# Layer 3 of a four-layer kernel: score copies by pairs of PSUM banks, softmax sums of the first sequence on TensorE, MLP steps regrouped

## The chip, the cores and the metric

The kernel runs on one core of a Trainium2 chip. A core has five engines that take their instructions in order, each from its own queue: TensorE (PE; its weight loads are listed apart as PEld), VectorE (DVE), ScalarE (ACT), GpSimd (POOL) and SyncE (SP), which here only issues DMAs. They wait for each other through semaphores. Data lie in SBUF (128 partitions) and in PSUM, which has eight banks of 2 KB per partition and takes the results of matmuls. The metric is the time of one execution on the device in microseconds (us), less being better. The kernel before took 3798.1 us, the median of three runs (3795.4 to 3805.48).

## The reference

Four layers in a row on x of shape 4 x 512 x 512 (four sequences of 512 positions): cross attention (layer 0), two recurrent layers (1 and 2), and layer 3, a resampler with an MLP. Everything is float32. The change is in layer 3:

```python
residual = latents                              # the output of layer 2, 4 x 512 x 512
h = concat([x, latents], axis=1)                # x is the context: 1024 keys per sequence
q = (latents @ q_w + q_b)                       # 16 heads of 32
kv = (h @ kv_w + kv_b)
attn = einsum('bkhd,bnhd->bhkn', q, kmat) / DH
attn = where(full_mask, attn, -inf)             # the mask is on the 512 context keys only
attn = softmax(attn)
attn_out = einsum('bhkn,bnhd->bkhd', attn, v) @ out_w + out_b + residual
out = rmsnorm(attn_out, postnorm_w)
out = gelu(out @ mlp_w1 + mlp_b1) @ mlp_w2 + mlp_b2     # 512 -> 2048 -> 512
return out + residual
```

## The kernel before, in words

Layers 0 to 2 fill the first 2398 us and are not touched, except that the pool of their weight buffers (`wpool`, four buffers of 8 KB per partition, line 36) is opened at the top of the kernel and is used by layer 3 too, through `load_w` (line 61).

Layer 3 (`layer3`, from line 1102) treats the four sequences b = 0 to 3 one after the other. The 16 heads of a sequence are four groups m of four heads. The four heads of a group sit in four row groups of TensorE and are computed together. A *unit* is (b, m, h), where h is one half of the 512 queries. The 1024 keys of a unit are eight blocks of 128, and a *turn* i works on two of them, so a unit has four turns (NS = 4), a group m has eight (PERIOD), a sequence 32, and there are 128 turns in all. In this text T0 to T3 are the turns i with i mod 4 = 0 to 3, and c = i mod 8 is the turn in its group.

The loop over turns (line 1414) is the order of work on TensorE, VectorE, ScalarE and GpSimd: nothing reorders it, each engine takes its own instructions in the order in which the loop writes them (`manual_schedule`), and semaphores follow from which tile an instruction reads or writes. SP's DMAs go as early as their buffers are free, in order. A turn has parts that belong to different blocks of keys, as a pipeline written out by hand:

- `scores(i)`: 16 matmuls (two per product in float32) into the PSUM tile `ps`, 4 x 2 x 256 columns, that is four banks, one for each head of the group. There is one such tile, so the next scores wait until all its readers are done.
- `largest(i)`: VectorE takes the maximum over the two blocks into `run`; on the first four blocks (the context) it adds the mask column `mc` as it does.
- `kept(i)`: ScalarE copies the scores to an SBUF tile `w` (six buffers), adding the mask column on the context blocks. It comes after `largest` and waits for it.
- In T0, for the unit that has just ended: `gathered` turns `run` on TensorE (`ptm`) and VectorE reduces it to `mx`; `spread` turns `mx` back over all partitions (`pb`) and ScalarE copies it to `mb`.
- `lowered(i-4)`: VectorE subtracts `mb` from `w`. `weights(i-4)`: ScalarE takes the exponential in place.
- a *tick*: VectorE writes a one-column tile and GpSimd copies it to `mark`, so that GpSimd does not pass that point earlier (lines 1449 to 1451).
- `added(i-5)`: GpSimd adds the two blocks of `w` to the accumulator `acc` (two buffers).
- `values(i-5)`: 16 matmuls of `w` with the values into `po`, one bank for both query halves.
- two turns after the last values of a unit: `counted` sums `acc` over the partitions with a matmul with ones (`pn`), and `divided` takes the reciprocal on VectorE and writes the result to `y`.

Beside these, a turn takes pieces of two generators (`taken`, line 1395). `early` prepares the next group: `prep` (projections q, k, k, v, v in five pieces), and, where the next group opens a new sequence, first `begin` (loads, four transposes `ptx` copied to `xT`, and four GpSimd additions of the output bias at line 1150). It runs at c = 0, 4 and 6, with two, two and three pieces. `rest` is `finish(b)`, the output projection, the norm and the MLP of the sequence before; it runs at the other five turns of a group, two pieces at a time. Its 38 pieces are: the output projection of each of four row tiles (`pout`), the normed transpose of a half of the rows (`ptn` to `nT`), and for each of two halves and four blocks of 512 hidden columns two pieces `ph` with gelu into `hT` (two buffers) and two pieces `po2` added to the residual. After four output pieces, the first `nT` shifts the pairs by one, so that in the first half of the rows a turn holds one `ph` and one `po2` piece or an `nT`, and in the second half both of a kind. When the last sequence's attention is done, the rest of its `finish` runs alone.

`ps_s` is a pool of three PSUM banks, used by everything that is neither `ps` nor `po`.

The instructions of `mm` (all projections and MLP matmuls) carry line 73, those of `columns` line 1293.

## Time and profile before

| what | value |
|---|---|
| median of three runs | 3798.1 us (3795.4 to 3805.48) |
| the profiled execution, its own time | 3804.08 us |
| its span, first to last instruction | 3802.2 us |
| mean granted TensorE clock | 0.95 |
| busy: PE, PEld | 3443.3 us (91%), 1972.7 us (52%) |
| busy: DVE, ACT, POOL | 2711.7 (71%), 1930.9 (51%), 1915.7 (50%) |
| layer 3 from its first scores | 2398.07 us to the end |

The span is what the engines' rows cover; the execution's own time is 1.9 us more. The page has the span in 40 slices of 95 us; a digit is the busy share in tenths. Times within layer 3 are given as us from the start of the span. In the rows of the timeline the columns are start, duration, engine, line, operation, the tile written and the tiles read, shapes and count, and in brackets the idle time before the instruction and the engine and tile that ended it. In the view of waits: who waited, for whom, us in total, times, longest.

### The profile page before, as it was taken

To read this page: it belongs to the slowest core of one execution; us is meant where nothing else is said; L and a number is where in the kernel's file an instruction comes from. 1 tells how busy PE (TensorE), PEld (TensorE's weight loads), DVE (VectorE), ACT (ScalarE), POOL (GpSimd) and SP (SyncE) were. 2 spreads that over 40 slices of the span, in tenths; PEclk is the share of its full clock that TensorE was granted. 3 is DMA by queue.
4 is the path that set the end of the run, shared out by engine and by line. 5 is a ranking of instruction groups with operands and counts; after the bars stand their busy time and mean duration, and the time that the engine had idled before them with its cause. 6 is when DMAs were issued, how large, how long until landed. Compare 5 with 4: busy or idle time off the path is not lost. (4 is left out here: it accounts for less than half of the span.)

```text
span 3802.2 us, 54498 instructions
## 1 busy us (share of the span) xinstructions
PE 3443.3 (91%) x21952; PEld 1972.7 (52%) x21952; DVE 2711.7 (71%) x3637; ACT 1930.9 (51%) x2758; POOL 1915.7 (50%) x1106
## 2 busy tenths in 40 slices
PE   9999999988999999999999977667789999989889
PEld 3333333465566666666666634334455555555456
DVE  6777777689988888888888861466666666566631
ACT  4777775534444444444444422355565566656531
POOL 4777776524444444444444432266654554554540
PEclk9999999999999999999999989688899999999999
DMA  4000000156677777777777764100022212212123
GB/s 151 24 12 23 12 9 20 34 146 142 147 178 177 178 187 178 177 178 177 174 176 177 180 155 103 43 10 23 15 71 88 81 45 92 67 59 73 62 94 122
DMA packets 188235, 385.75 MB, mean 101 GB/s; under 512 B 18064, under 2 KB 44816, under 8 KB 185936
## 3 DMA queue, kind: packets, MB, share of 16 engines
q1 hardware_dynamic: 149680, 250.67, 20.4%
q0 software_dynamic: 38304, 131.61, 19.0%
q8 instruction: 173, 2.83, 0.3%
q14 instruction: 78, 0.64, 0.1%
HBM read 246.45 MB, written 4.19 MB: 66 GB/s over the span
## 5 line engine op out<-in xcount | busy, mean ns | idle before, releaser
L292 POOL TENSOR_TENSOR aT<-aT,nmT 128x1536 f32<-128x1536 f32 x124 | 428.5, 3460 | 208.1 <-ACT aT L290 184.8
L1288 POOL TENSOR_TENSOR acc<-acc,w 128x1024 f32<-128x1024 f32 x192 | 491.5, 2560 | 7.8 <-POOL mark L1451 0.2
L254 DVE CUSTOM_DVE_ANT_0 sc<-psc,nm 128x512 f32<-128x512 f32 x512 | 354.1, 692 | 148.0 <-PE psc L242 90.3
L871 DVE TENSOR_TENSOR ry<-kv,o_r 128x1024 f32<-128x1024 f32 x256 | 397.7, 1594 | 7.2 <-PE pm L73 0.5
L1451 POOL COPY mark<-tick 128x1 f32<-128x1 f32 x128 | 92.7, 724 | 556.9 <-DVE tick L1450 378.1
L1276 ACT ACTIVATE w<-w 128x2048 f32<-128x2048 f32 x128 | 244.5, 1911 | 200.4 <-DVE w L1272 187.7
L1272 DVE TENSOR_TENSOR w<-w,mb 128x2048 f32<-128x2048 f32 x128 | 321.5, 2522 | 1.8 <-ACT mb L1265 1.8
L866 DVE TENSOR_TENSOR_SCAN kv<-W,kv 128x1032 f32<-128x1032 f32 x128 | 296.4, 2315 | 0.2 <-DMA kv<-A 0.2
L584 POOL DMA_DIRECT2D kv<-A x127 | 111.5, 878 | 360.6 <-DVE kv L839 227.6
L290 ACT COPY aT<-pst 128x512 f32<-128x512 f32 x372 | 196.5, 595 | 178.6 <-PE pst L279 178.1
L73 PE MATMUL ph<-nT,l_m 128*128 128x256 f32 x1024 | 240.7, 393 | 18.0 <-DVE nT L1357 18.0
L73 PE MATMUL po<-l_m,hT 128*128 128x512 f32 x512 | 238.2, 611 | 18.8 <-ACT hT L1374 18.8
L298 ACT ACTIVATE aT<-aT 128x2048 f32<-128x2048 f32 x128 | 246.8, 1929 | 5.6 <-POOL aT L292 4.9
L1293 PE MATMUL po<-w,v 128*32 128x256 f32 x2048 | 160.1, 437 | 84.4 <-ACT w L1276 48.3
L73 PEld LDWEIGHTS ph<-nT,l_m 128*128 128x128 f32 x1024 | 199.3, 197 | 61.9 <-DVE nT L1357 19.2
L279 PE MATMUL pst<-q,km 32*128 32x512 f32 x1024 | 206.5, 640 | 9.4 <-DVE mxs L254 5.8
L1236 DVE TENSOR_TENSOR run<-ps,run 128x1024 f32<-128x1024 f32 x128 | 156.5, 1223 | 77.4 <-PE ps L1199 75.2
L1199 PE MATMUL ps<-q,kT 32*128 32x256 f32 x2048 | 170.1, 453 | 40.2 <-ACT w L1220 32.5
L1383 DVE TENSOR_TENSOR x<-po,x 128x512 f32<-128x512 f32 x64 | 44.2, 691 | 223.3 <-PE po L73 223.3
L242 PE MATMUL psc<-km,q 32*128 32x512 f32 x1024 | 198.9, 653 | 0.8 <-ACT q L223 0.8
L1220 ACT ACTIVATE w<-ps,mc 128x1024 f32<-128x1024 f32 x128 | 135.6, 1110 | 118.0 <-DVE tick L1450 62.0
L885 PE MATMUL py<-ry,k 128*32 128x512 f32 x1024 | 161.6, 627 | 36.0 <-DVE ry L871 24.3
(268 smaller groups left out, 7311.8 us busy)
## 6 DMA issues: line engine op xcount, KB each, us to landing
l_m<-in_L_W SPq DMA_DIRECT2D x64, 1024.0 KB, 5.0
kv<-A POOLq DMA_DIRECT2D x127, 516.0 KB, 6.1
L_wk<-in_L_Wk SPq DMA_DIRECT2D x16, 1024.0 KB, 7.9
L_wr<-in_L_Wr SPq DMA_DIRECT2D x16, 1024.0 KB, 7.1
L_wv<-in_L_Wv SPq DMA_DIRECT2D x16, 1024.0 KB, 5.8
L_wg<-in_L_Wg SPq DMA_DIRECT2D x16, 1024.0 KB, 7.9
L_wo<-in_L_Wo SPq DMA_DIRECT2D x64, 256.0 KB, 4.9
L_fk<-in_L_fWk SPq DMA_DIRECT2D x16, 1024.0 KB, 6.6
```

Source lines behind the costliest of these rows:

```text
L73: nc.tensor.matmul(ps, lhsT, rhs, start=(i == 0), stop=(i == len(pairs) - 1))
L242: nc.tensor.matmul(psc, d["q"][g][rs, lt * P : (lt + 1) * P], d["km"][rs, a, :], start=True, stop=True, tile_position=(32 * r, 0),)
L254: nc.vector.tensor_tensor_reduce(sc, ps[r], d["nm"][lt], 1.0, -3.0e38, ALU.add, ALU.max, mxs[:, a, lt, c : c + 1])
L279: nc.tensor.matmul(pst, d["km"][rs, a, s * P : (s + 1) * P], d["q2", a][rs, :], start=True, stop=True, tile_position=(32 * r, 0),)
L290: nc.scalar.copy(w[:, r, :], pst)
L292: nc.gpsimd.tensor_tensor(w[:, n:, :], w[:, n:, :], nmT[:, None, :].to_broadcast([P, NR - n, L]), ALU.add)
L298: nc.scalar.activation(w, w, AF.Exp)
L866: nc.vector.tensor_tensor_scan(flat(kv), flat(W[g % 2]), flat(kv), 0.0, ALU.mult, ALU.add)
L871: nc.vector.tensor_tensor(y, kv[:, 4 * h : 4 * h + 4, None, :TP].to_broadcast([P, 4, 2, TP]), d["r"][:, i].rearrange("p (o m) -> p o m", o ...
L1272: nc.vector.tensor_tensor(w, w, mb, ALU.subtract)
L1276: nc.scalar.activation(w, w, AF.Exp)
L1288: nc.gpsimd.tensor_tensor(d["acc", m, h], d["acc", m, h], w[:, :, e, :], ALU.add)
```

## The change

- The tile `ps` is read by pairs of its four banks: `largest` takes two half maxima for each pair, and `kept` is called twice, for the upper pair ahead of `lowered` and `weights`, for the lower pair after `largest`. The copy no longer adds the mask; the exponential does, as a bias, on the context blocks. `w` has seven buffers.
- `scores` comes first in a turn, and `values` and `added` are a turn later (VAL is 6, not 5).
- In sequence 0 the exponentials are summed on TensorE: `values` has a second set of 16 matmuls with `ones` into `pn`, which is held through the unit; `added`, `counted` and the tick are left out there, and `divided` comes in the turn of the last values. In the other sequences `counted` and `divided` come seven turns behind the last scores, as before, with `counted` ahead of `values`; `acc` has one buffer.
- The pieces of `finish` are larger: two output projections, the first `nT`, and then a whole `ph` block (`hidden`) or a whole `po2` block (`closed`), one in a turn. The second `nT` follows the first `hidden`. In the last sequence the `hidden` of the next block comes ahead of `closed`. `hT` has one buffer (in the last sequence it takes buffers of `w`), `nT` two.
- Which turn takes which piece is written out in `turns` and `ready`: for sequences 1 to 3 `prep` at c = 0, 0, 4, 6, 6 (at 2, 2, 4, 6, 6 where the next sequence is begun; its `begin` is at c = -1 and 0, two transposes each), in sequence 0 at 1, 2, 4, 6, 7.
- `wpool` is opened later and closed with layer 2; layer 3 has its own three weight buffers (`wp`).

```diff
-    wpool = ctx.enter_context(tc.tile_pool(name="w", bufs=NW))
...
-                    if k % 2:
+                    if k == 1:
                         yield
                 for x in xn[b]:
                     nc.gpsimd.tensor_tensor(x, x, ob, ALU.add)
+                yield
...
-            def kept(i):
+            def kept(i, c):
+                (b, m, h), j = place(i)
+                if i not in ws:
+                    ws[i] = sp.tile([P, NR, 2, HQ], F32, tag="w", name="w", bufs=7)
+                nc.scalar.copy(
+                    ws[i][:, c : c + 2].rearrange("p r e q -> p (r e q)"),
+                    st[b]["ps"][:, c : c + 2].rearrange("p r e q -> p (r e q)"),
+                )
...
-                run = d["run"]
-                for e in range(2):
-                    mc = d["mc"][:, s + e : s + e + 1]
-                    if a:
-                        nc.vector.tensor_tensor(run, ps[:, :, e, :], run, ALU.max)
...
+                for c in range(0, NR, 2):
+                    ps, run = d["ps"][:, c : c + 2], d["run"][:, c : c + 2]
+                    for e in range(2):
+                        mc = d["mc"][:, s + e : s + e + 1]
+                        if a:
+                            nc.vector.tensor_tensor(run, ps[:, :, e, :], run, ALU.max)
+                        elif j or e:
+                            nc.vector.scalar_tensor_tensor(run, ps[:, :, e, :], mc, run, ALU.add, ALU.max)
+                        else:
+                            nc.vector.tensor_scalar(run, ps[:, :, e, :], mc, None, ALU.add)
...
+            def ticked(i):
+                if 0 <= i - VAL < NU and units[(i - VAL) // NS][0]:
+                    tick = sp.tile([P, 1], F32, tag="tick", name="tick")
+                    nc.vector.memset(tick, 0.0)
+                    nc.gpsimd.tensor_copy(mark, tick)
...
             def weights(i):
-                w = ws[i].rearrange("p r e q -> p (r e q)")
-                nc.scalar.activation(w, w, AF.Exp)
+                (b, m, h), j = place(i)
+                w = ws[i]
+                a, s = divmod(2 * j, LT)
+                if a:
+                    w = w.rearrange("p r e q -> p (r e q)")
+                    nc.scalar.activation(w, w, AF.Exp)
+                else:
+                    for e in range(2):
+                        nc.scalar.activation(
+                            w[:, :, e, :], w[:, :, e, :], AF.Exp, bias=st[b]["mc"][:, s + e : s + e + 1]
+                        )
...
-                    d["acc", m, h] = sp.tile([P, NR, HQ], F32, tag="acc", name="acc", bufs=2)
+                    d["acc", m, h] = sp.tile([P, NR, HQ], F32, tag="acc", name="acc", bufs=1)
...
+                if b == 0 and j == 0:
+                    d["pn"] = ps_s.tile([P, HQ], F32, tag="s", name="pn")
                 for e in range(2):
+                    ends = dict(start=(j == 0 and e == 0), stop=(j == NS - 1 and e == 1))
+                    columns(po[:, h, :], lambda r: v[:, 2 * j + e, 32 * r : 32 * r + 32], lambda r: w[:, r, e, :], **ends)
+                    if b == 0:
+                        columns(d["pn"], lambda r: ones, lambda r: w[:, r, e, :], **ends)
...
+                def normed(h):
+                    nT = nTs[h] = sp.tile([P, KC, T2], F32, tag="nT", name="nT", bufs=2)
...
+                def hidden(h, j):
+                    nT = nTs[h]
+                    m1 = load_w(t["L3_W1"][:, j * C : (j + 1) * C], f"l3_m1_{j}", wp)
+                    if b < B - 1:
+                        hT = sp.tile([P, KC, T2], F32, tag="hT", name="hT", bufs=1)
+                    else:
+                        hT = sp.tile([P, NR, 2, HQ], F32, tag="w", name="hT", bufs=7)[:, :, 0, :]
+                    hTs[h, j] = hT
+                    for m in range(0, KC, 2):
+                        pm = ps_s.tile([P, 2, T2], F32, tag="s", name="ph")
+                        for e in range(2):
+                            mm(pm[:, e, :], [(m1[:, k, (m + e) * P : (m + e + 1) * P], nT[:, k, :]) for k in range(KC)])
+                        for e in range(2):
+                            i = j * KC + m + e
+                            nc.scalar.activation(hT[:, m + e, :], pm[:, e, :], AF.Gelu_apprx_tanh, bias=b1[:, i : i + 1])
+                def closed(h, j):
+                    hT = hTs.pop((h, j))
+                    m2 = load_w(t["L3_W2"][j * C : (j + 1) * C, :], f"l3_m2_{j}", wp)
+                    for i in range(2):
+                        lt = 2 * h + i
+                        pm = ps_s.tile([P, C], F32, tag="s", name="po2")
+                        mm(pm, [(hT[:, k, i * P : (i + 1) * P], m2[:, k, :]) for k in range(KC)])
+                        nc.vector.tensor_tensor(xn[b][lt], pm, xn[b][lt], ALU.add)
...
+                scaled(aos[-1], before)
+                normed(0)
+                yield
+                blocks = [(h, j) for h in range(2) for j in range(4)]
+                for n, at in enumerate(blocks):
+                    if b < B - 1:
+                        hidden(*at)
+                        if n == 0:
+                            normed(1)
+                        yield
+                    else:
+                        if n == 0:
+                            hidden(*at)
+                            normed(1)
+                        if n + 1 < len(blocks):
+                            hidden(*blocks[n + 1])
+                    closed(*at)
                     yield
...
-            LOW, VAL, CNT = NS, NS + 1, NS + 3
+            VAL = NS + 2
...
+                for c in (0, 1, 3, 5, 7) if opens or not nxt else (1, 2, 3, 5, 7):
+                    ready.add(base + c)
...
+                if opens:
+                    gen = begin(nxt[0])
+                    for c in (-1, 0):
+                        turns.setdefault(base + c, []).append(gen)
+                gen = prep(*nxt)
+                for c in (1, 2, 4, 6, 7) if b == 0 else (2, 2, 4, 6, 6) if opens else (0, 0, 4, 6, 6):
+                    turns.setdefault(base + c, []).append(gen)
+            ready.update(range(NU, NU + VAL))
...
+            wp = opened("l3w", 3)
...
+                if i < NU:
+                    scores(i)
+                if last:
+                    gathered(last)
+                if over and over[0]:
+                    counted(over)
                 if 0 <= i - VAL < NU:
                     values(i - VAL)
+                if last:
+                    spread(last)
                 if i < NU:
+                    kept(i, 2)
+                if 0 <= low < NU and not last:
                     lowered(low)
+                    ticked(i)
                     weights(low)
                 if i < NU:
                     largest(i)
+                    kept(i, 0)
+                if last:
                     lowered(low)
+                    ticked(i)
                     weights(low)
+                if 0 <= i - VAL < NU and units[(i - VAL) // NS][0]:
                     added(i - VAL)
                 if over:
+                    divided(over)
...
+        wpool = both.enter_context(tc.tile_pool(name="w", bufs=NW))
```

## The prediction, made before the changed kernel was run

> **What bounds the kernel now.** I read the slices of the page first, then busy time by stage, then what TensorE waited for in each stage, then the timeline of single turns. The slices say that TensorE is the busy engine, with a dip of busy time and of granted clock where layer 3 begins (slices 26 to 29 of 40):
>
> ```profile
> PE   9999999988999999999999977667789999989889
> PEclk9999999999999999999999989688899999999999
> ```
>
> The stages come from the first score matmuls of each unit. In order: sequence 0, 1, 2, 3, the drain after the last scores, the last MLP (columns: PE, PEld, DVE, ACT, POOL busy, then granted clock, DMA share, GB/s).
>
> ```profile
> 2398.07:2670.82 272.75, 175.49 (x1410) 103.84 (x1409) 173.81 (x156) 131.87 (x103) 154.77 (x80) 0.75 0.06 18
> 2670.82:2988.41 317.59, 281.86 (x1957) 174.87 (x1953) 205.56 (x197) 185.70 (x173) 175.82 (x101) 0.94 0.18 59
> 2988.41:3310.96 322.55, 297.47 (x2021) 184.31 (x2017) 208.14 (x201) 191.14 (x180) 172.62 (x100) 0.97 0.22 72
> 3310.96:3620.43 309.47, 271.00 (x1845) 164.27 (x1841) 201.68 (x193) 180.85 (x166) 161.89 (x93) 0.95 0.20 67
> 3620.43:3668.64 48.21, 41.05 (x229) 24.83 (x225) 18.65 (x20) 20.98 (x20) 33.30 (x17) 0.92 0.26 83
> 3668.64:3802.20 133.56, 128.16 (x436) 81.33 (x432) 19.77 (x34) 20.13 (x45) 7.13 (x8) 0.99 0.34 116
> ```
>
> Sequence 0 has no MLP beside it: no engine is above 65% and the clock is 0.75. TensorE's waits there sum to 97 us; the three largest, then three of sequence 2 (whose waits sum to 25; sequences 1 and 3 have 36 and 38):
>
> ```profile
> PE ps L1199 <- ACT w L1220: 30.2, 7, 10.9
> PE ptm L1249 <- DVE tick L1450: 19.7, 7, 3.4
> PE po L1293 <- DVE y L1323: 16.4, 5, 4.8
> ...
> PE po L73 <- ACT hT L1374: 6.3, 4, 2.9
> PE ph L73 <- DVE nT L1357: 5.4, 1, 5.4
> PE ptx L1145 <- ACT xT L1146: 4.9, 1, 4.9
> ```
>
> So sequence 0 goes at the pace of a chain (scores, maxima, copy, next scores); sequences 1 to 3 go at TensorE's pace, 88 to 92% busy. Five rows carry the rest: scores after a short and values after a long idle (1.15 against 1.94; both kinds take about 1.1 at full clock); ACT's copy waiting for a POOL sum that holds its buffer; two subtractions back to back, and the POOL mark that cannot run beside the second.
>
> ```profile
> 2547.35 1.15 PE L1199 MATMUL ps<-q,kT 32*128 32x256 f32 x16 [2.47 <-ACT w L1220]
> 2553.34 1.94 PE L1293 MATMUL po<-w,v 128*32 128x256 f32 x16 [4.83 <-DVE y L1323]
> 2655.92 1.86 ACT L1217 COPY w<-ps 128x2048 f32<-128x2048 f32 x1 [4.12 <-POOL acc L1285]
> 3067.20 4.49 DVE L1272 TENSOR_TENSOR w<-w,mb 128x2048 f32<-128x2048 f32 x2
> 3069.57 2.17 POOL L1451 COPY mark<-tick 128x1 f32<-128x1 f32 x1 [3.56 <-DVE tick L1450]
> ```
>
> **The change, part by part.** I call the four turns of a unit T0 (the one that also turns the last unit's maxima), T1, T2, T3.
>
> *Pairs of banks.* Today the copy waits for both maxima though it needs neither (the copy at 3077.36 starts when they end): the score tile is held for 2.5 + 2.1 us. With pairs the two engines swap halves. Four maxima of 512 columns cost about 0.73 each (rows of 128x512 out of PSUM: 0.69; 128x1024: 1.28), 2.9 for 2.5; two copies 1.04 for 1.87. The mask moves from copy to exponential: two of 1.1 for one of 1.91 in half the turns. All of that is on DVE and ACT, 65 and 59% busy in sequences 1 to 3, and counts there only where it stands in the chains below.
> [...]
>
> *Sequence 0.* The sums go to TensorE: 16 more matmuls a turn, 1.0 at full clock, 1.94 cold. POOL drops out, and the subtraction is 2.28 instead of up to 3.4 beside POOL. One unit at full clock: T0: scores 1.1, turning ready with both reductions 3.1, values and sums until 4.1, spread and its copies 5.9, upper copy 6.95, upper maxima 8.4; next scores 8.55. T1: subtraction until 10.7, exponentials 12.95, upper copy 14.0, second exponentials 16.15, lower copy 17.2: 8.75 long. T2 6.1, T3 5.4: 28.8, and about 1.4 for the evictions of the projections: 30.2. The first two units have no projections, so idles near 4 us and a cold clock: 31.5. Now: 272.75 / 8 = 34.1. Saved: 272.75 - (2 x 31.5 + 6 x 30.2) = 28. Bounds: 45 saved (nothing of the evictions or the clock shows), 13 lost (cold throughout: T0 4.5 longer, the others 1 each, 36 a unit).
>
> *Start.* The first maxima wait until 2405.18 for a DMA that shares their buffer; the weight pool's place changes that: 0 to 7 saved, I take 3.
>
> *Sequences 1 to 3: what is removed.* Whole MLP steps per turn: no wait for hT, nT, ptx (16.6 of sequence 2's 25). Table loads fall from 73 to about 50, 23 x 1.28 = 29 us of ACT, hidden behind TensorE. [...]
>
> *What is added.* The POOL sums now run six turns behind the scores, not five, but the count is still due seven behind. So the sum of the fourth block starts in T1, and the count stands in T2 ahead of the values; one accumulator instead of two is free by then. From T0's first score: reductions 3.1, spread copied 4.9, upper copy 5.95, upper maxima 7.4, subtraction and tick 9.7, second subtraction (the mark waits) 11.95, two adds (4.80) 16.75. T1's copy needs the buffer which these adds read (seven buffers, freed six turns later): 17.8; exponentials (two, 2.15) 20.0, lower copy 21.1, scores of T2 at 21.2. The fourth block's adds end at 21.7, before the count is reached at 22.3. TensorE's own work in T0 and T1 is 20.1 with two projections (turns 0 and 1: 4.0 + 6.95 + 9.15) and 16.6 with one (turns 4 and 5). So it idles 1.1 and 4.6 us; after the second it is cold: 0.94 + 0.87 by scores 2.09 for 1.15 and values 1.94 for 1.07. With T2 9.75 and T3 9.15 a full group of eight turns is 40.1 + 41.9 = 82, against 80.1 measured. Where there is no MLP piece, T2 ends at 27.1 and T3 at 34.4. Where the next sequence is begun, four POOL additions (4.96) stand between the two sums: 7 to 8 more. Group by group, us:
> sequence 1: 68.75, 83.98, 80.21, 84.65 becomes 76.4, 84.3, 82.2, 90.7 (+16);
> sequence 2: 75.05, 84.17, 80.13, 83.20 becomes 79.6, 80.4, 82.2, 90.7 (+10);
> sequence 3 (to 3630.61): 74.44, 83.64, 80.43, 81.14 becomes 79.6, 80.4, 82.2, 74 (-3). Together +23.
> One thing is a matter of 0.1 us: in T1 with a first MLP half, the third subtraction is ready at 19.4 and the second add of the last block starts at 19.25. If the subtraction is first, the sums end at 24.0 and the count waits 1.8: at most 24 units, 43 us; half the units have it, and I take half of those: +11.
>
> *Drain.* Now 3630.61 to 3668.64, 38 us, ended by POOL. One turn later the three last blocks' sums wait for a tick behind the fourth subtraction, which stands behind two MLP evictions at 29.5 to 30.2: 32.5 + 3 x 4.8 = 47, and the next matmuls are cold, +2: +11 (0 to 14).
>
> *Last MLP.* 128 of 133.6 us busy; running a block ahead saves the last 1 to 3: -1.
>
> *Moved DMAs.* Three weight buffers instead of four on SP's queue: a load lands in 5.0 and has two steps of 6.9 in the last MLP, 18 elsewhere. One hT instead of two: its reader ran a turn before. Nothing; gone only if a load took over 13 us.
>
> Sum: -28 - 3 + 23 + 11 + 11 - 1 = +13 on the span of 3802.2 (3804.08 with what lies around it, 6 above the median of the three runs, 3798.1). Predicted 3798 + 13 = 3811.
>
> **Rivals.**
> *Faster.* The mark gets in between the two subtractions. For it: marks of 0.18 where DVE waits in between. Against: 2.17 wherever the subtractions are back to back, as here. The chain is 2.2 shorter, T2 starts at 19: idle 0 and 2.4, the latter too short to cool, 5.1 a group, 12 groups: -61, 3750. It decides from 0.6 us off the chain (two units in each of 12 groups, 14 us).
> *Slower by the port.* The subtraction is first in every unit: +32 on the forecast, 3843. For it: subtractions of 3.4 and adds of 6.88 for two. Against: the 0.15 us.
> *Sequence 0 stays cold:* +41, 3852. For it: 0.75 now. Against: a third more matmuls in less time.
> *The pairs are not independent*, the copy and the maxima still take turns on the whole tile: 1.5 later in each T0 of 24 units, 1.4 a turn in sequence 0: +36 + 45, 3892. Against: the banks are whole (each head group is 2 KB).
>
> **How the numbers follow.** Forecast 0.40, faster rival 0.29, port 0.15, cold 0.09, pairs 0.04, others 0.03. A difference under 0.3% (11.4 us) can hardly be told from none: 3786.7 to 3809.5 is "same". The forecast's own range is 3790 to 3830, and 0.18 of it and its neighbours lies in that band. Faster: 0.30; slower: 0.52. The range for 8 in 10 leaves out the pairs above and the far part of the faster rival with a larger gain in sequence 0 below: 3750 to 3865.
>
> **What would show it.** Units of sequence 0 near 30 us. In sequences 1 to 3 the score matmuls of T2 waiting some 4 us for ACT's w in turn 6 and 1 in turn 2, or the count waiting for POOL's acc; no waits for hT, nT, ptx; a drain that ends with POOL, near 48 us. I am wrong if T0 and T1 take under 20.6 us together, or if sequence 0 keeps 34 us a unit.

## The result, and the profile after

The changed kernel takes 3906.8 us (median of four runs, 3902.8 to 3913.4); the kernel before takes 3800.0 on the same chip (four runs). The ratio is 1.028, with a 95% interval of 1.026 to 1.030: 107 us slower, outside the predicted range of 3750 to 3865. The profiled execution took 3913.4 us, its span is 3911.7.

From the page of the changed kernel, the two rows of slices that answer to those shown of the kernel before:

```profile
PE   9999999988999999999999776677898888988889
PEclk9999998989999999999999887888999899989889
```

The digits of TensorE's busy share in sequences 1 to 3 (from the 29th slice on), mostly 9 before, are now mostly 8, and its clock has more 8s there. By stage, with the same columns as before (span of the stage, then PE, PEld, DVE, ACT, POOL busy, clock, DMA share, GB/s):

```profile
2407.57:2683.31 275.74, 185.91 (x1737) 109.53 (x1736) 177.81 (x189) 134.80 (x133) 7.85 (x5) 0.81 0.05 14
2683.31:3029.26 345.95, 299.62 (x2049) 181.55 (x2049) 212.04 (x257) 179.48 (x198) 137.31 (x83) 0.93 0.18 58
3029.26:3384.29 355.03, 305.35 (x2001) 186.76 (x2000) 210.55 (x264) 182.06 (x201) 165.86 (x100) 0.91 0.19 63
3384.29:3717.90 333.61, 281.46 (x1849) 167.75 (x1848) 202.98 (x255) 174.46 (x191) 156.00 (x93) 0.91 0.19 62
3717.90:3778.73 60.83, 44.69 (x256) 25.87 (x256) 21.36 (x24) 21.69 (x23) 33.19 (x18) 0.81 0.24 78
3778.73:3911.70 132.97, 127.76 (x436) 81.12 (x432) 19.86 (x34) 20.14 (x45) 7.13 (x8) 0.99 0.36 119
```

Against the rows of before: sequence 0 +3.0, sequences 1 to 3 +28.4, +32.5 and +24.1, the drain +12.6, the last MLP -0.6, and 9.5 before the first scores; together the 109.5 by which the spans differ. So 85 of it lies in sequences 1 to 3. There TensorE's busy time rose by 36 us for nearly the same work (a colder clock, 0.91 to 0.93 for 0.94 to 0.97) and its idle time by 49.

What TensorE waited for from 2670.82 to 3620.43 (sequences 1 to 3) in the kernel before; the columns are us in total, times, longest:

```profile
PE po L1293 <- ACT w L1276: 28.4, 19, 7.2
PE po L1293 <- DVE y L1323: 19.7, 11, 5.1
PE po L73 <- ACT hT L1374: 18.8, 12, 2.9
PE ph L73 <- DVE nT L1357: 16.3, 3, 5.5
PE ptx L1145 <- ACT xT L1146: 9.9, 2, 4.9
...
PE ps L1199 <- ACT w L1220: 2.3, 1, 2.3
```

And in the changed kernel, the same three sequences (2683.31 to 3717.9):

```profile
PE ps L1199 <- ACT w L1214: 133.5, 40, 9.8
PE pn L1305 <- POOL acc L1300: 5.6, 1, 5.6
PE ptx L1144 <- ACT hT L1378: 3.9, 1, 3.9
PE po L72 <- ACT hT L1378: 1.9, 1, 1.9
```

Nearly everything that the change set out to remove is gone: the waits of the MLP (hT, nT, ptx: 45.0 us, now 5.8) and those of the values for exponentials and for y (48.1 us, now none). In their place stands one wait that hardly existed, 133.5 us in which the scores wait for ScalarE's copies (L1214). One unit of sequence 2 shows how it comes about (timeline of the changed kernel; start, duration, engine, line, operation, and in brackets the idle time before it and what ended it):

```profile
3247.48 1.15 PE L1199 MATMUL ps<-q,kT 32*128 32x256 f32 x16
...
3249.25 1.29 DVE L1245 TENSOR_REDUCE mx<-ptm 128x4 f32<-128x512 f32 x2 [0.97 <-PE ptm L1244]
...
3251.27 1.07 ACT L1260 COPY mb<-pb 128x512 f32<-128x512 f32 x2 [6.53 <-PE pb L1255]
3252.23 1.03 ACT L1214 COPY w<-ps 128x1024 f32<-128x1024 f32 x1
3253.29 0.75 DVE L1235 TENSOR_SCALAR run<-ps,mc 128x512 f32<-128x512 f32 x1 [2.75 <-ACT w L1214]
...
3256.19 4.50 DVE L1267 TENSOR_TENSOR w<-w,mb 128x2048 f32<-128x2048 f32 x2
3256.31 1.01 ACT L1214 COPY w<-ps 128x1024 f32<-128x1024 f32 x1 [3.05 <-DVE run L1233]
3257.37 1.15 PE L1199 MATMUL ps<-q,kT 32*128 32x256 f32 x16 [2.27 <-ACT w L1214]
...
3258.56 2.17 POOL L1274 COPY mark<-tick 128x1 f32<-128x1 f32 x1 [16.94 <-DVE tick L1273]
...
3260.69 4.77 POOL L1300 TENSOR_TENSOR acc<-acc,w 128x1024 f32<-128x1024 f32 x2
...
3265.49 1.01 ACT L1214 COPY w<-ps 128x1024 f32<-128x1024 f32 x1 [4.22 <-POOL acc L1300]
...
3266.40 2.19 ACT L1286 ACTIVATE w<-w,mc 128x1024 f32<-128x1024 f32 x2
3266.53 2.98 DVE L1233 SCALAR_TENSOR_TENSOR run<-ps,mc,run 128x512 f32<-128x512 f32 x4 [5.84 <-ACT w L1214]
...
3269.55 1.01 ACT L1214 COPY w<-ps 128x1024 f32<-128x1024 f32 x1 [0.97 <-DVE run L1233]
...
3270.61 2.09 PE L1199 MATMUL ps<-q,kT 32*128 32x256 f32 x16 [3.99 <-ACT w L1214]
```

Three things are to be seen.
- In T0 (3247.48) VectorE has its reductions done at 3250.54 and then idles 2.75 us. Its maxima of the *lower* pair wait for ScalarE's copy of the *upper* pair, which stands behind the two copies of mb. The lower copy in turn waits for all four maxima. So the copy and the maxima still take turns: 1.03, then four maxima, then 1.01.
- In T1 (3257.37) the upper copy waits for GpSimd's adds, whose tensor still occupies its w buffer, until 3265.49. All four maxima now stand behind that copy, and the lower copy behind them.
- The scores of T2 start 23.1 us after those of T0, after 4 us of idle, and take 2.09 us instead of 1.15 (this is what "cold" means below).

### The profile page after: what moved, and what is told of

Same layout as the page of the kernel before. It is cut to its first block, busy times and chain, and to the rows that moved or that the text cites. A ratio compares the mean times of both kernels' runs of the same rounds, so it can differ in the third digit from the quotient of the medians.

```text
span 3911.7 us, 55513 instructions
## 1 busy us (share of the span) xinstructions
PE 3495.7 (89%) x22400; PEld 1992.5 (51%) x22400; DVE 2732.6 (70%) x3859; ACT 1912.8 (49%) x2862; POOL 1717.4 (44%) x1016
## 5 line engine op out<-in xcount | busy, mean ns | idle before, releaser
L1214 ACT COPY w<-ps 128x1024 f32<-128x1024 f32 x256 | 259.4, 1013 | 411.9 <-PE ps L1199 138.5
L1199 PE MATMUL ps<-q,kT 32*128 32x256 f32 x2048 | 179.2, 472 | 224.2 <-ACT w L1214 224.2
L1300 POOL TENSOR_TENSOR acc<-acc,w 128x1024 f32<-128x1024 f32 x144 | 340.7, 2366 | 5.8
L1267 DVE TENSOR_TENSOR w<-w,mb 128x2048 f32<-128x2048 f32 x128 | 300.3, 2364 | 1.8 <-ACT mb L1260 1.8
L1274 POOL COPY mark<-tick 128x1 f32<-128x1 f32 x94 | 63.0, 670 | 522.1 <-DVE tick L1273 519.4
L1199 PEld LDWEIGHTS ps<-q,kT 32*128 32x128 f32 x2048 | 108.7, 218 | 301.6 <-ACT w L1214 267.8
L1233 DVE SCALAR_TENSOR_TENSOR run<-ps,mc,run 128x512 f32<-128x512 f32 x192 | 141.3, 750 | 147.3 <-ACT w L1214 142.8
L72 PE MATMUL po<-l_m,hT 128*128 128x512 f32 x512 | 228.9, 600 | 1.9 <-ACT hT L1378 1.9
L72 PEld LDWEIGHTS ph<-nT,l_m 128*128 128x128 f32 x1024 | 196.9, 195 | 43.3 <-issue 13.1
L1231 DVE TENSOR_TENSOR run<-ps,run 128x512 f32<-128x512 f32 x256 | 170.8, 688 | 61.5 <-ACT w L1214 56.8
L1305 PE MATMUL po<-w,v 128*32 128x256 f32 x2048 | 178.2, 464 | 3.1 <-ACT w L1283 3.1
```

Source lines behind the costliest of these rows:

```text
L72: nc.tensor.matmul(ps, lhsT, rhs, start=(i == 0), stop=(i == len(pairs) - 1))
L1199: nc.tensor.matmul(ps[:, r, e, :], d["k", m][rs, a, (s + e) * P : (s + e + 1) * P], d["q", m][rs, h * HQ : (h + 1) * HQ], start=True, stop ...
L1214: nc.scalar.copy(ws[i][:, c : c + 2].rearrange("p r e q -> p (r e q)"), st[b]["ps"][:, c : c + 2].rearrange("p r e q -> p (r e q)"),)
L1233: nc.vector.scalar_tensor_tensor(run, ps[:, :, e, :], mc, run, ALU.add, ALU.max)
L1267: nc.vector.tensor_tensor(w, w, mb, ALU.subtract)
L1300: nc.gpsimd.tensor_tensor(d["acc", m, h], d["acc", m, h], w[:, :, e, :], ALU.add)
```

## The experiments

I asked first which of the two, the turn-taking on one tile (theory A, with the w buffer as its second half) or the rest of the change (theory C: MLP turns, sums, clock), costs the time. The lengths of sequences below are differences between the first scores of units in each trace; the last sequence is taken to the scores of its last turn.

| kernel | median, us | ratio to before, 95% | sequence 0 | sequences 1 to 3 |
|---|---|---|---|---|
| before | 3800 to 3804 | 1 | 272.8 | 949.6 |
| changed | 3906.8 | 1.028 (1.026 to 1.030) | 275.7 | 1034.6 |
| two tiles | 3812.4 | 1.0027 (1.0017 to 1.0036) | 241.8 | 975.1 |
| adds a turn earlier | 3803.0 | 1.0005 (0.9996 to 1.0015) | 275.2 | 941.1 |
| both | 3720.3 | 0.978 (0.977 to 0.980) | 241.8 | 889.0 |
| whole tile | 3776.0 | 0.993 (0.992 to 0.995) | 235.6 | 943.1 |
| whole tile, adds earlier | 3714.3 | 0.977 (0.975 to 0.978) | 236.9 | 888.6 |
| T0: maxima first | 3793.5 | 0.9975 (0.9966 to 0.9985) | 248.4 | 948.6 |
| both, and T0: maxima first | 3700.6 | 0.974 (0.972 to 0.975) | 225.0 | 884.8 |

**Two tiles.** The scores' four banks become two tiles, one for each pair:

```diff
-                ps = ps_w.tile([P, NR, 2, HQ], F32, tag="w", name="ps")
+                ps = [ps_w.tile([P, 2, 2, HQ], F32, tag=f"w{c}", name=f"ps{c}") for c in range(2)]
...
-                            ps[:, r, e, :],
+                            ps[r // 2][:, r % 2, e, :],
...
-                    st[b]["ps"][:, c : c + 2].rearrange("p r e q -> p (r e q)"),
+                    st[b]["ps"][c // 2].rearrange("p r e q -> p (r e q)"),
...
-                    ps, run = d["ps"][:, c : c + 2], d["run"][:, c : c + 2]
+                    ps, run = d["ps"][c // 2], d["run"][:, c : c + 2]
```

> The scores' four banks are two tiles of two banks, so that a copy of the one and the maxima of the other have nothing in common; all else is as in the changed kernel (3906.8 us). Theory A (the pairs share one tile, so copy and maxima take turns; and T1's upper copy waits for a w buffer that GpSimd's adds still read): a turn of sequence 0 loses up to one copy (1.01 us) and part of the maxima's 2.98; units 34.5 -> about 30, -34 us; in sequences 1 to 3 T0 to T2 goes from 23.1 to about 21.2, -1.9 x 24 = -46 us, the buffer's wait stays: 3825 us (3800 to 3850). Theory B (the buffer alone sets sequences 1 to 3): only sequence 0 gains, 3872. Theory C (the MLP's new turns, the sums on TensorE or the clock cost the time): within 10 us of 3906.8.

Measured: 3812.4 us, 94 less than the changed kernel. Sequence 0 lost 34 us, to 30.2 a unit, and sequences 1 to 3 lost 59; theory C is out as the main cause. The instructions are the same, only what waits for what is not. It shows in what ended the idle time of ScalarE before its copies (view of line L1214; us, times), first in the changed kernel, then with two tiles:

```profile
  DVE run L1233: 128.7, 62
  POOL acc L1300: 84.5, 22
  DVE run L1231: 49.4, 54
...
  POOL acc L1300: 90.0, 23
...
  DVE run L1233: 0.7, 1
```

The waits for VectorE's maxima (L1233, L1231) are gone but for one, those for GpSimd's adds stay.

**Adds a turn earlier.**

```diff
-                if 0 <= i - VAL < NU and units[(i - VAL) // NS][0]:
+                if 0 <= i - VAL + 1 < NU and units[(i - VAL + 1) // NS][0]:
                     tick = sp.tile([P, 1], F32, tag="tick", name="tick")
...
-                    d["acc", m, h] = sp.tile([P, NR, HQ], F32, tag="acc", name="acc", bufs=1)
+                    d["acc", m, h] = sp.tile([P, NR, HQ], F32, tag="acc", name="acc", bufs=2)
...
-                if 0 <= i - VAL < NU and units[(i - VAL) // NS][0]:
-                    added(i - VAL)
+                if 0 <= i - VAL + 1 < NU and units[(i - VAL + 1) // NS][0]:
+                    added(i - VAL + 1)
```

> GpSimd's adds of a block (and their tick) stand one turn earlier in sequences 1 to 3, so that the w buffer that T1's upper copy takes was left a turn before; a second acc buffer goes with it; pairs as in the changed kernel. Theory A: the 4.2 us of waiting for the adds in T1 go, T0 to T2 23.1 -> about 19, at most the 40 to 48 us a sequence that the scores wait for copies now: -25 us in each of three sequences, sequence 0 unchanged: 3832 us (3800 to 3860). If the pairs alone cost the time (theory P): within 15 us of 3906.8. If the adds now run into DVE's work elsewhere (the port): 3920 or more.

Measured: 3803.0 us, 104 less; sequence 0 is unchanged, as it has no adds. The same place of a unit of sequence 2, with T0's scores at 3187.71 (timeline of this kernel):

```profile
3200.91 4.82 POOL L1300 TENSOR_TENSOR acc<-acc,w 128x1024 f32<-128x1024 f32 x2
3201.40 1.00 ACT L1214 COPY w<-ps 128x1024 f32<-128x1024 f32 x1
...
3202.43 2.98 DVE L1233 SCALAR_TENSOR_TENSOR run<-ps,mc,run 128x512 f32<-128x512 f32 x4 [1.51 <-ACT w L1214]
...
3208.37 1.15 PE L1199 MATMUL ps<-q,kT 32*128 32x256 f32 x16
```

The copy of T1 starts 13.7 us after T0's first scores, not 18.0, while the adds are still running, and T2 starts 20.7 after T0 with no wait and in 1.15 us. The buffer's wait is real and worth about as much as the tiles.

**Both.** The two edits together.

> Two tiles and early adds together. Theory A: sequence 0 -34 us, each later sequence -35 of its 40 to 48 us of waits: 3768 us (3740 to 3800), faster than the kernel before. Theory C: within 10 us of 3906.8. If one of the two waits hides the other, as much as the better one of the two alone.

Measured: 3720.3 us, better than the expected 3740 to 3800. The two gains nearly add up (94 + 104 against 187). In this kernel one sees the swap that the change was written for: in T1 of the first unit of sequence 0 VectorE's maxima and ScalarE's copies go side by side (timeline):

```profile
2412.93 3.06 DVE L1233 SCALAR_TENSOR_TENSOR run<-ps,mc,run 128x512 f32<-128x512 f32 x4 [1.78 <-PE ps L1199]
2413.41 2.10 ACT L1214 COPY w<-ps 128x1024 f32<-128x1024 f32 x2 [2.66 <-PE ps L1199]
```

None of them is longer than alone. The rows are merged ones and hold short idle times between their parts; by the views of the lines L1233 and L1214, the median is 0.751 us a maximum and 1.012 a copy both here and in the changed kernel.

**Whole tile.** The pairs undone, all else of the change kept:

```diff
-                nc.scalar.copy(
-                    ws[i][:, c : c + 2].rearrange("p r e q -> p (r e q)"),
-                    st[b]["ps"][:, c : c + 2].rearrange("p r e q -> p (r e q)"),
-                )
+                nc.scalar.copy(
+                    ws[i].rearrange("p r e q -> p (r e q)"),
+                    st[b]["ps"].rearrange("p r e q -> p (r e q)"),
+                )
...
-                for c in range(0, NR, 2):
-                    ps, run = d["ps"][:, c : c + 2], d["run"][:, c : c + 2]
-                    for e in range(2):
...
+                ps, run = d["ps"], d["run"]
+                for e in range(2):
...
-                if i < NU:
-                    kept(i, 2)
```

> The pairs undone: two maxima over the whole tile, then one copy over the whole tile, as before the change; masks still added in the exponentials, sums of sequence 0 still on TensorE, the MLP's turns, seven buffers and the turn of the adds as in the changed kernel. Theory A: sequence 0 stays at 34 to 35 us a unit (the pairs gave nothing there); in sequences 1 to 3 the maxima no longer stand behind the copy that waits for GpSimd, T0 to T2 23.1 -> 21.2: 3865 us (3850 to 3890). If the pairs did gain a little and the loss lies in the other parts (theory C): 3910 to 3940.

Measured: 3776.0 us, 131 less than the changed kernel and faster than the kernel before. The expectation was wrong by 89, and in a telling place: sequence 0 went to 29.5 us a unit, not 34 to 35. The pairs had not merely failed to gain there; they cost. That could not be the length of the work: two maxima and a copy (2.60 + 1.86) and copy, four maxima, copy (1.01 + 2.98 + 1.01) differ by 0.5 us a turn, at most 17 over the 32 turns. By turns, it was T0 that had grown (11.5 against 8.9 in sequence 0) and T1 (8.7 against 6.8). Hence a second theory: in T0 the order of instructions is what costs. The upper copy stands behind the copies of mb, and the maxima, which before the change ran while mb was on its way, now stand behind the upper copy.

**T0: maxima first.** The changed kernel with that one move, still on one tile:

```diff
-                if i < NU:
+                if i < NU and not last:
                     kept(i, 2)
...
                 if i < NU:
                     largest(i)
+                    if last:
+                        kept(i, 2)
                     kept(i, 0)
```

> The changed kernel (3906.8 us) with one move, in T0 alone: both of its copies come behind its maxima, so that the maxima need not wait for ScalarE's upper copy, which stands behind the two copies of mb from the gathering of the unit before. Theory T0 (the order in T0 costs it): T0 11.7 -> about 9 us in sequence 0 and 11.1 -> 9.4 in the others: -23 and -45 us, 3838 us (3815 to 3860). If only the taking of turns within a tile matters, and not what stands ahead of the upper copy: 3885 to 3907.

Measured: 3793.5 us, 113 of the 131. More than expected, because the delay in T0 is passed on. The same stretch of a unit of sequence 2, T0's scores at 3170.99 (timeline of this kernel):

```profile
3172.76 1.29 DVE L1245 TENSOR_REDUCE mx<-ptm 128x4 f32<-128x512 f32 x2 [0.97 <-PE ptm L1244]
3173.96 0.74 DVE L1235 TENSOR_SCALAR run<-ps,mc 128x512 f32<-128x512 f32 x1
...
3176.85 4.49 DVE L1267 TENSOR_TENSOR w<-w,mb 128x2048 f32<-128x2048 f32 x2
...
3181.35 4.77 POOL L1300 TENSOR_TENSOR acc<-acc,w 128x1024 f32<-128x1024 f32 x2
...
3186.15 1.01 ACT L1214 COPY w<-ps 128x1024 f32<-128x1024 f32 x1 [4.22 <-POOL acc L1300]
```

The maxima follow the reductions with no idle; the subtractions start 5.9 us after T0's scores instead of 8.7, so the adds start 10.4 after them instead of 13.2, and T1's copy, which waits for those adds, 15.2 instead of 18.0. The remaining 18 us to the whole tile, 13 of them in sequence 0, lie mostly in the other turns, where copies and maxima still alternate (10 of the 13 in T1 and T2). The 113 us of this move, the 94 of the two tiles and the 104 of the early adds are not parts of one sum: each shortens the same chain, and all three together give 206, as a later run shows.

**Whole tile, adds earlier.** The two edits shown above, together.

> The whole-tile kernel (pairs undone, 3776.0 us) with GpSimd's adds a turn earlier. Theory A: T1's one copy no longer waits for the adds; T1 to T3 lose the 1 to 3 us by which they stand over 9.5 in sequences 1 to 3 (T2 is 12.9, 11.4 and 10.4 there), and the drain about 8 us: 3731 us (3705 to 3750). If two tiles of pairs are worth something of their own in sequences 1 to 3, it stays above the 3720 of both edits together; if one tile does as well, it is at or below it. If the wait for the buffer is only a matter of the pairs: 3776.

Measured: 3714.3 us, within 6 us of the two tiles with early adds (3720.3). With the w buffer free in time, splitting the score tile as the change orders it buys nothing over one whole copy behind two whole maxima.

**Both, and T0: maxima first.** Two tiles, early adds and the move in T0.

> Two tiles and early adds (3720.3 us), and in T0 both copies behind the maxima. If the upper maxima of T0 still wait for the upper copy behind the mb copies, which costs about 2 us of T0 and T1 in sequence 0 and little later, where TensorE is busy: 3705 us (3698 to 3712), below the 3714.3 of the whole tile with early adds. If two tiles have nothing left to give: 3714 to 3722.

Measured: 3700.6 us, 0.974 of the kernel before (0.972 to 0.975). This is the best version found, 206 us below the change. Here the split does pay, 14 us against the whole tile, 12 of it in sequence 0, and 8 of these in its first unit (21.6 us for 29.6), whose turns hold nothing but scores, maxima and copies. What is left in sequences 1 to 3 is mostly TensorE's own work: its busy time there is 282.80 of 292.17, 289.73 of 304.31 and 267.86 of 288.35 us.

The other runs ask what the rest of the change is worth.

**Before, with masks and sums.** The kernel before, with the mask in the exponential (so one copy a turn) and sequence 0's sums on TensorE:

```diff
-                if a:
-                    nc.scalar.copy(w.rearrange("p r e q -> p (r e q)"), ps.rearrange("p r e q -> p (r e q)"))
-                else:
-                    for e in range(2):
-                        nc.scalar.activation(
-                            w[:, :, e, :], ps[:, :, e, :], AF.Identity, bias=d["mc"][:, s + e : s + e + 1]
-                        )
+                nc.scalar.copy(w.rearrange("p r e q -> p (r e q)"), ps.rearrange("p r e q -> p (r e q)"))
...
+                if b == 0 and j == 0:
+                    d["pn"] = ps_s.tile([P, HQ], F32, tag="s", name="pn")
...
+                    if b == 0:
+                        columns(d["pn"], lambda r: ones, lambda r: w[:, r, e, :], **ends)
```

> The kernel before (3802 us) with only two parts of the change: masks added in the exponentials, so that each turn has one whole copy, and sequence 0's sums on TensorE. If these two are what brought sequence 0 from 272.8 us to the 235.6 of the whole-tile kernel: -37 us, 3765 us (3755 to 3775), and the rest of the change (the MLP in turns of one kind, values and adds a turn later, seven buffers) is worth what lies between this and 3776, a loss of some 10 us. If sequence 0 owes it to the later values: 3795 to 3802.

Measured: 3792.3 us (0.9972, 0.9963 to 0.9982). Sequence 0 lost 6 us, not 37. Masks and sums alone are not what brought it to 29.5 a unit.

**The whole tile, with GpSimd's sums in sequence 0.** The second half of the edit above taken back in the whole-tile kernel (tick, adds and count in all sequences).

> The whole-tile kernel (3776.0 us) with sequence 0's sums back on GpSimd, as in the other sequences. If the sums on TensorE are what shortened sequence 0 (no ticks, no adds beside VectorE, a higher clock): units 29.5 -> 33 or 34, +30 to +37 us: 3810 us. If the masks in the exponentials did it: 3770 to 3782.

Measured: 3824.9 us, 49 more; sequence 0 takes 285.6 us at a clock of 0.73. So in that frame the sums on TensorE are worth 49 us, but not for the reasons I gave alone: with the adds a turn later, GpSimd's sums bring T1's wait for the w buffer into sequence 0 as well, as one of its turns shows (timeline of this kernel):

```profile
2508.70 6.92 POOL L1299 TENSOR_TENSOR acc<-acc,w 128x1024 f32<-128x1024 f32 x2
...
2515.65 1.86 ACT L1214 COPY w<-ps 128x2048 f32<-128x2048 f32 x1 [4.29 <-POOL acc L1299]
...
2517.57 2.09 PE L1199 MATMUL ps<-q,kT 32*128 32x256 f32 x16 [8.57 <-ACT w L1214]
```

**Scores first.** The kernel with masks and sums, and `scores(i)` moved ahead of `gathered` and `values`:

```diff
+                if i < NU:
+                    scores(i)
                 if i >= NS and i % NS == 0 and i <= NU:
                     gathered(units[i // NS - 1])
...
-                if i < NU:
-                    scores(i)
```

> The kernel before with masks in the exponentials and sequence 0's sums on TensorE (3792.3 us), and with one part more of the change: the scores come first in a turn, ahead of gathering and values. Theory T0: in e7 T0 of sequence 0 takes 11.7 us, because its scores wait behind the turning of the last unit's maxima, its reductions and the values; with the scores first it falls to about 9: -22 us there, and up to 0.5 in each of 24 later units: 3760 us (3745 to 3772). If sequence 0 owes its 235.6 us in the whole-tile kernel to the values a turn later: 3785 to 3798.

Measured: 3789.4 us, and T0 of sequence 0 at 13.1 us: the theory fell. The timeline shows two projections, pieces of `prep`, behind one another in T0, so that the next scores come late whatever the order ahead of them (T0's scores were at 2463.90):

```profile
2470.76 3.70 PE L73 MATMUL pq<-xT,w3q 128*128 128x512 f32 x8 [0.24 <-ACT mb L1258]
...
2474.30 3.60 PE L73 MATMUL pk<-cT,w3k 128*128 128x512 f32 x8
...
2477.83 1.15 PE L1199 MATMUL ps<-q,kT 32*128 32x256 f32 x16
```

**Prep spread.** On top of that, in groups 1 and 2 of sequence 0, `prep` one piece a turn as in the change:

```diff
+                if g in (1, 2):
+                    taken(early, 1 if c in (1, 2, 4, 6, 7) else 0)
-                if c in (0, 4, 6):
+                elif c in (0, 4, 6):
                     taken(early, 3 if c == 6 else 2)
```

> The kernel before with masks in the exponentials, sums of sequence 0 on TensorE and scores first (3789.4 us); in groups 1 and 2 of sequence 0 prep's five pieces lie one each in the turns c = 1, 2, 4, 6, 7, as in the change, not two, two and three in c = 0, 4 and 6. If the bunched pieces are why T0 of sequence 0 stayed at 13.3 us: units 2 to 5, now 31.2 + 38.3 + 33.4 + 38.3 = 141.2, come to about 131, as with the values early and the whole tile: 3779 us (3772 to 3785). If not: 3785 to 3797.

Measured: 3784.2 us. Units 2 to 5 came to 32.0 + 33.7 + 30.9 + 33.8 = 130.4 us, as expected: the bunched projections were what held T0 (13.1 us on average, now 10.2). The 95% intervals of this kernel's ratio to before (0.9935 to 0.9970) and of the last one's (0.9959 to 0.9979) overlap, so for the whole kernel a gain is not shown.

**Values early.** The whole tile with early adds, values five turns behind the scores as before the change, too:

```diff
-            VAL = NS + 2
+            VAL = NS + 1
...
-                for b0, at in ((True, i - VAL), (False, i - VAL - 1)):
+                for b0, at in ((True, i - VAL), (False, i - VAL - 2)):
```

> The whole-tile kernel with the adds early (3714.3 us), and the values too: both five turns behind the scores, as before the change; the count stays seven behind. What is left between this and the kernel before is then sums, masks, scores first and the MLP's turns. If values a turn later are worth something (TensorE waits for exponentials of the turn before): 3725 to 3745. If they are worth nothing: 3708 to 3720.

Measured: 3744.1 us. Values a turn later are worth 30 us, 16 of them in sequence 0. With them early, the waits of values for exponentials are back in sequences 1 to 3 (11.1 us in 21 times, against none), so it is the later turn that removes these. The waits for y do not come back, so those went for another reason.

The runs make a ladder from the kernel before to the change: 3802; masks and sums 3792; scores first 3789; prep spread (two groups) 3784; the MLP's turns and what goes with them, prep's other turns and seven buffers, 3744; values a turn later 3714; adds a turn later 3776; pairs on one tile 3907. The steps from 3792 to 3789 and 3784 are within the noise: the intervals of these three kernels overlap. The step of 40 us was not taken apart.

## Why the prediction was wrong, and where it was right

**The step that failed** is the first one: "With pairs the two engines swap halves." They do not, as long as the two pairs are one tile: each engine's read of it waits for the other engine's read before it in the order of the program, whichever banks they touch. ScalarE idled 178.1 us for VectorE's maxima before its copies in the changed kernel, and 0.7 with two tiles. The two-tile kernel is the one that the prediction described, and its terms fit that one: in 18 of the 24 units of sequences 1 to 3 T2 starts 20.6 us after T0 (21.2 forecast, 23.1 measured in the changed kernel), the count waits 12.1 us for GpSimd (+11), sequences 1 to 3, to the turning of the last maxima, take 28.2 us more (+34), drain and last MLP 8.7 more (+10), and sequence 0 31 less (-28). It took 3812.4 us against the 3811 forecast, and some of that is luck. The errors of single terms partly cancel, in sequence 0 too: its first two units took 11.6 us less than forecast (25.7 for 31.5 each, on average), the other six 9.1 more (31.7 for 30.2). What the shared tile adds to the changed kernel is 94 us. The rival "The pairs are not independent" had the right mechanism and a fair price (81 us on the forecast; 3892 for a measured 3907), and was given 4 chances in 100 because "the banks are whole". That reason answers whether the hardware could read both pairs at once. It can, as the kernel with two tiles and early adds shows: its maxima of 2412.93 and its copies of 2413.41 overlap, with medians of 0.751 and 1.012 us as in the changed kernel. The question was what the semaphores follow, and the text ahead of the prediction said it: from which tile an instruction reads or writes.

The trace of before held a hint, too. Its copy waited for the maxima though both only read, and the prediction quoted that as the loss to be removed, without asking what made two readers wait for each other (in layer 3 of before, ScalarE idled 53.9 us for the maxima of L1238 ahead of its copies of L1220). Why two readers are put in order at all, no run here shows. What the runs show is how far the order reaches: over the whole tile of four banks in the changed kernel, while with tiles of two banks the same reads went side by side.

**A mis-sized place within it.** The rival's price was sought in the wrong proportions: 36 us in later sequences and 45 in sequence 0, where two tiles gave back 59 and 34. The run with T0's maxima first shows why: "1.5 later in each T0" did not reckon that the lower maxima too would stand behind the copies of mb (2.75 us of idle VectorE), and that the subtractions, the mark and GpSimd's adds are all later by that much, which T1's copy then waits for.

**T1's wait for the w buffer** was right in its place and its rows: mark 2.17, two adds 4.77 (4.80 forecast), T2 cold at 2.09. But it lasted longer: the adds ended 18.0 us after T0's scores, not 16.75, the upper copy 19.0, not 17.8, and T2 started at 23.1, not 21.2. So 1.2 us are T0's delay passed on and 1.0 is ScalarE's idle time before the lower copy, which waits for the maxima behind the upper one; the rest was 0.3 shorter than forecast. What was missed is that this was a choice of the change that an edit can undo: the adds need not be a turn later because the values are. Early adds are worth 104 us to the change, 92 with two tiles, 62 with the whole tile. The count, for which the forecast had 11 us, was late only once here (5.6 us).

**Sequence 0** keeps 34.5 us a unit, one of the two signs that the prediction named for its own error; the other (T0 and T1 under 20.6 us together) did not show: 23.4 on average. The bounds given for sequence 0 do not follow from their own terms: units of 28.8 us would save 42, not 45, and units of 36.3 lose 18, not 13. Nothing hangs on it, as 3 were lost.

**The MLP's waits** vanished as forecast (45.0 to 5.8 us in three sequences), table loads fell from 74 to 50 (1.28 us each in both traces), the last MLP gained 0.6 for 1, and no new wait for a weight load appeared. In the changed kernel TensorE only reached the scores earlier and waited there. What it is worth once the scores' chain is shorter lies within the step of 40 us above and was not measured by itself.

**The drain**: 49.2 us from the turning of the last maxima to `pout`, forecast about 49, ended by GpSimd as said (waits of the changed kernel between 3717.9 and 3778.73):

```profile
PE pn L1305 <- POOL acc L1300: 13.1, 2, 10.9
```

**The start** was forecast at -3, and the first scores came 9.5 us later. Over the ten kernels with the new pool they started at 2397.7 to 2407.6, over the four with the old one at 2398.1 to 2403.5. The mean differs by 2 us, so most of the 9.5 belongs to this one execution, and no gain or loss of the start itself is shown. The wait for the DMA stayed, but was shorter: the first read of the scores came 4.7 to 4.9 us after the first scores in the ten kernels, 7.0 to 7.6 in the four. That this is the pool's doing is not shown.

**The split's own price.** Four half maxima cost 2.98 us for 2.60 on the context blocks and 2.74 for 2.48 on the others, near the forecast 2.9 for 2.5. With the tiles separate and the adds early the split was worth nothing as long as T0 kept the change's order (3720.3 us, for 3714.3 with the whole tile), and 14 us without it (3700.6), so the order in T0 weighed more than this price.

## What to carry to other kernels

Splitting an instruction by halves made two engines independent here only when the halves were separate tiles (94 us between the two kernels): what waited for what followed the tile, not the bytes, and two readers counted. When a pipeline stage moves a turn later, ask for each part of it whether it must move too; here the values gained by it and the adds, moved along with them, held a buffer that the critical copy needed. And where an instruction is moved ahead, look at what stands in front of it on its own engine and who has to wait behind it: one copy placed behind two small ones in one turn of four was worth 113 us.

## What the runs showed of the hardware

- In these runs VectorE and ScalarE did not slow each other by reading different PSUM banks at the same time: the median of a 128x512 maximum with the mask column is 0.751 us and that of a 128x1024 copy 1.012, in the changed kernel, where they take turns, and with two tiles and early adds, where many overlap.
- One subtraction on VectorE of 128x2048 took 2.28 us in the median of the changed kernel and 4.47 beside one of GpSimd's adds. The 4.47 was in the two-tile kernel, where it began 0.03 us after an add (timeline from 3194.3 on):

```profile
3194.34 2.35 POOL L1300 TENSOR_TENSOR acc<-acc,w 128x1024 f32<-128x1024 f32 x1
3194.37 4.47 DVE L1267 TENSOR_TENSOR w<-w,mb 128x2048 f32<-128x2048 f32 x1
```

  The add keeps its time, and the subtraction is longer by 2.19 us, nearly the whole add. In the changed kernel one that began 0.9 us before the end of an add took 3.05. It goes the other way, too: in the run with GpSimd's sums two adds took 6.92 for 4.77, with a subtraction beside the second that took its usual 2.28. So in these rows one of the two waits for the other, and they do not share the loss. "The port" in the prediction and in the expectation of the early adds is the author's name for such waits; what lies behind them is not shown.
- Waits cost twice here: in the changed kernel all 19 scores after more than 4 us of idle TensorE take 2.09 us for 1.15, and 36 of the 85 us lost in sequences 1 to 3 are longer busy time, not idle time.
